# A second self-attention in stretches of scores, projections, scores and values on four double banks, with its ends and cross-attention's last element in another order

## The chip, the cores and the metric

The kernel runs on one core of one Trainium2 chip, in float32 throughout. Its time is the device time of one launch in microseconds (us). Three runs of the kernel before took 2361.93, 2363.57 and 2368.61 us; the median is 2363.57. A further execution was recorded by the hardware profiler: it took 2357.97 us, of which 2356.2 are the span from its first to its last instruction.

## What is computed

Two transformer blocks follow each other on x, 8 elements of 512 rows and 256 columns. The change is in the second block: its self-attention, and both ends of the cross-attention behind it.

```python
def _attn(xq, ctx, wq, wkv, wo, bo):          # H = 16 heads of DH = 64
    q = _heads(xq @ wq)
    k, v = jnp.split(ctx @ wkv, 2, axis=-1)
    k = _heads(k)
    v = _heads(v)
    sq, cq = _sincos(q.shape[2], DH)
    sk, ck = _sincos(k.shape[2], DH)
    q = _rope(q, sq, cq)
    k = _rope(k, sk, ck)
    sim = jnp.einsum('bhnd,bhmd->bhnm', q, k) * DH ** (-0.5)
    a = jax.nn.softmax(sim, axis=-1)
    o = jnp.einsum('bhnm,bhmd->bhnd', a, v)
    o = o.transpose(0, 2, 1, 3).reshape(xq.shape[0], xq.shape[1], MID)
    return o @ wo + bo
...
attn_in = _adaln(x, cond, ln1_w, ln1_b, g1_w, g1_b, b1_w, b1_b)
x = _attn(attn_in, attn_in, sa_wq, sa_wkv, sa_wo, sa_bo) + x
cross_in = _adaln(x, cond, ln1_w, ln1_b, g1_w, g1_b, b1_w, b1_b)
ctx_n = _ln(context, ca_lnc_w, ca_lnc_b)
x = _attn(cross_in, ctx_n, ca_wq, ca_wkv, ca_wo, ca_bo) + x
ffn_in = _adaln(x, cond, ln2_w, ln2_b, g2_w, g2_b, b2_w, b2_b)
h = jax.nn.gelu(ffn_in @ ff_w1 + ff_b1, approximate=False)
x = h @ ff_w2 + ff_b2 + x
```

## The kernel before

The kernel runs in stages on one core: the first block (its self-attention, cross-attention and feed-forward interleaved), then the second block's self-attention (class of work `batch4`, L991), then its cross-attention (`cross`, L1372) and its feed-forward (`feed_forward`, L1412). Almost every matrix product is issued in the helper `mm` (L117, L118), so the profile gives all of them one line; they are told apart by their tiles. In these stages TensorE, VectorE (DVE), ScalarE (ACT) and GpSimd (POOL) run in the order in which the program records their instructions (`manual_schedule`). The queue of SyncE (SP), which issues most DMAs, is ordered by the planner.

**Forms of a product.** TensorE's array holds 128 rows and 128 columns. A product over all of it is shown as `128*128`. Scores use it as four row strips, `32*128`: four heads, each with 32 of its 64 dimensions (the even or the odd half of the rotation), side by side. Values use column strips, `128*64`: two heads side by side. The sums of a softmax are `128*32`, four side by side. A float32 product is recorded as two matmuls.

**A group** is four heads, g = 0 to 3 for each element b. For each group there are queries and keys (`turned`, L1008: two products of 512 columns each into two PSUM banks; VectorE multiplies each by the cosine and the sine table into four tiles of tag t, L1016 and L1017; GpSimd combines them, L1019 and L1020), four blocks of scores by keys (`score(g, kt)`, L1028: eight matmuls into two double banks, and an exponential of 1024 columns each on ScalarE, L1037, into tiles p, of which there are six), and four blocks of values (`value(g, kt)`, L1039, four matmuls of 64 columns each into banks O and D). The sums over keys are first added up elementwise: p0 + p1 on GpSimd (L1052), then p2 and p3 on VectorE (L1056). `sums` (L1066) reduces them over partitions by a product with ones; ScalarE copies them, and they go through DRAM into another layout (`sums_back`), where VectorE inverts them (`inverse`, L1082), and through DRAM again, broadcast (`inverse_back`, rb). `scaled` (L1099) multiplies the values' output oT by them, both halves on GpSimd. `out_tiles` (L1104) projects the eight oT of an element.

**The order.** `slots` (L1161) goes through 64 slots of two score blocks. A slot issues a score block, then what the dictionaries `steps` and `mid` hold for it (projections, norm of the next element, output projection), then the next score block, then two value blocks, then what `after` holds (sums, the transposition of the next element by `transposed`, L423, through two X banks). After the last slot come the last sums, eight products for the values of cross-attention (`cross_values`, L973, one bank, one copy and one DMA of 256 KB each into v_d), the norms of the first elements, and the output projection of the last element.

**PSUM.** One pool serves the whole kernel: two double banks S, one bank each O and D, two banks X (L99 to L115).

**DRAM and SyncE.** `load_vb` (L965) reads back the values of one element for cross-attention from v_d into the tile kv or vb. The weights of the feed-forward, `ff_w1` and `ff_w2`, are loaded into the places of `ca_wv4` and `sa_wo` when these have had their last use.

**Cross-attention.** `cross` goes through j = 0 to 7 for each element b: scores in two halves (j = 0 and 4), queries six ahead, output of the element before (`cross_out(b - 1, t)`, j from 5), sums and inverse. The last element has no queries to go ahead with. Then `feed_forward` does four double products with Gelu (`up`) and four output tiles (`down`) an element; the last cross-attention output stands behind the first element's.

Of the kernel before, what the change touches and what calls it, by code (L numbers as in the profile page):

```python
# [10 lines left out]
F32 = mybir.dt.float32  # L11
# [76 lines left out]
def fast_path(ctx: ExitStack, tc: tile.TileContext, a: dict, out: bass.AP):  # L88
# [7 lines left out]
    psum = ctx.enter_context(tc.tile_pool(name="psum", bufs=2, space=bass.MemoryType.PSUM))  # L96
    turns, extra = [0], []

# [874 lines left out]
    def cross_values(wk, p):  # L973
        ps = bank_x()
        for k in range(2):
            mm(ps, cross["v"][:, k, p * P : (p + 1) * P], ctxzT[:, k, :], k == 0, k == 1)
        v = wk.tile([P, N], F32, tag=f"k{p % 2}", name="v")
        nc.scalar.copy(v, ps)
        nc.sync.dma_start(v_d[:, p], v.rearrange("p (b t) -> p b t", b=B))


    with tc.tile_pool(name="ph4", bufs=2) as wk:
# [3 lines left out]
        steps, mid, after = {}, {}, {}  # L986

        def last(slot, fn):
            steps.setdefault(slot, []).append(fn)

        def batch4(b):  # L991
            s = {}
            base = 2 * NG * b

            def turn():
                s["hT"] = transposed(nk, s["z"], b, a1, b1, 1)

            def values(half, ts):
                if ts[0] == 0:
                    s["v", half] = wk.tile([P, NT, 512], F32, tag="v", name="v")  # L1000
                for t in ts:
                    ps = bank_x()
                    for k in range(2):
                        mm(ps, s["hT"][:, k, t * P : (t + 1) * P], w_sv[:, k, half * 512 : (half + 1) * 512],
                           k == 0, k == 1)
                    nc.scalar.copy(s["v", half][:, t, :], ps)

            def turned(g, w, tag, pss=None):  # L1008

                even, odd = pss or (bank_x(), bank_x())  # L1010
                for e, ps in enumerate((even, odd)):
                    for k in range(2):
                        mm(ps, w[:, k, (2 * g + e) * P : (2 * g + e + 1) * P], s["hT"][:, k, :], k == 0, k == 1)
                ec, es, oc, os = (wk.tile([P, N], F32, tag="t", name="t", bufs=4) for _ in range(4))
                for ps, c, sn in ((even, ec, es), (odd, oc, os)):
                    nc.vector.tensor_tensor(c, ps, rope_c, ALU.mult)  # L1016
                    nc.vector.tensor_tensor(sn, ps, rope_s, ALU.mult)  # L1017
                s[tag, g] = r = [wk.tile([P, N], F32, tag=f"{tag}{e}", name=f"{tag}{e}") for e in range(2)]
                nc.gpsimd.tensor_tensor(r[0], ec, os, ALU.subtract)  # L1019
                nc.gpsimd.tensor_tensor(r[1], es, oc, ALU.add)  # L1020

            def queries(g, pss=None):
                turned(g, w_sq, "q", pss)

            def keys(g, pss=None):
                turned(g, w_sk, "k", pss)

            def score(g, kt):  # L1028
                pss = [bank_s() for _ in range(2)]
# [9 lines left out]
            def value(g, kt):  # L1039
                if kt == 0:  # L1040
                    s["o", 0], s["o", 1] = bank_o(), bank_d()
                for u in range(2):
                    p = 2 * g + u
                    for i in range(2):
                        lo = (p % 4) * P + 64 * i
                        mm(s["o", u][64 * i : 64 * i + 64, :], s["v", p // 4][:, kt, lo : lo + 64],
                           s["p", g, kt, u][:, i, :], kt == 0, kt == NT - 1)

                if kt == 0:
                    for u in range(2):  # L1050
                        s["sm", g, u] = sm = wk.tile([P, 2, N], F32, tag="sm", name="sm", bufs=4)
                        nc.gpsimd.tensor_tensor(sm, s["p", g, 0, u], s["p", g, 1, u], ALU.add)  # L1052
                if kt == 2:
                    for t in (2, 3):
                        for u in range(2):
                            nc.vector.tensor_tensor(s["sm", g, u], s["sm", g, u], s["p", g, t, u], ALU.add)  # L1056
                if kt == NT - 1:
                    for u in range(2):
                        s["oT", 2 * g + u] = o = wk.tile([P, N], F32, tag="oT", name="oT", bufs=10)
                        nc.scalar.copy(o, s["o", u])  # L1060


            def queue(g):
                return nc.scalar if (b, g) == (B - 1, NG - 1) else nc.sync

            def sums(g):  # L1066

                d = bank_x()
# [5 lines left out]
                queue(g).dma_start(dd, den.rearrange("(j r) n -> j r n", j=4)[:, 0, :])  # L1074
                if (b, g) != (B - 1, NG - 1):
                    sums_back(g)

            def sums_back(g):
                s["rec", g] = rec = wk.tile([P, 4 * N // P], F32, tag="rec", name="rec")
                queue(g).dma_start(rec, flat(s["dd", g]))  # L1080

            def inverse(g):  # L1082
                rec = s["rec", g]
                nc.vector.reciprocal(rec, rec)
                s["inv", g] = d = dram.tile([4, N], F32, tag="rec_d", name="rec_d")
                queue(g).dma_start(flat(d), rec)
                check(rec)
                if (b, g) != (B - 1, NG - 1):
                    inverse_back(g)

            def inverse_back(g):
                d = s["inv", g]
                for u in range(2):
                    s["rb", g, u] = rb = wk.tile([P, N], F32, tag="rb", name="rb", bufs=3)
                    for e in range(2):
                        queue(g).dma_start(rb[64 * e : 64 * e + 64, :],
                                           d[2 * u + e : 2 * u + e + 1, :].to_broadcast([64, N]))

            def scaled(g, engines=None):  # L1099
                for u, eng in enumerate(engines or [nc.gpsimd] * 2):  # L1100
                    o = s["oT", 2 * g + u]
                    eng.tensor_tensor(o, o, s["rb", g, u], ALU.mult)  # L1102

            def out_tiles(qp):  # L1104
                project_out(qp, lambda k: s["oT", k], w_so, 8, add_to(b))

            if b:

                pieces = normed_in_pieces(nk, b, EPS1, lambda z: s.update(z=z))
                last(base - 8, pieces[0])  # L1110
                last(base - 6, pieces[1])
                after[base - 6] = [pieces[2]]
                last(base - 5, lambda: add_row(b, row("sabo")))
                after.setdefault(base - 4, []).append(turn)
                last(base - 3, lambda: queries(0))
# [1182 lines left out]
```

## Time and profile before

| what | value |
|---|---|
| median of three runs | 2363.57 us |
| profiled execution | 2357.97 us |
| its span | 2356.2 us |
| first block, from 0 to | 826.7 us |
| second self-attention | 826.7 to 1814.0 us |
| cross-attention and feed-forward | 1814.0 to 2356.2 us |
| granted TensorE clock, mean | 0.999 |

Engine time in the stretch of the second self-attention, 827 to 1814 us:

| engine | busy us | instructions |
|---|---|---|
| TensorE | 985.51 | 4705 |
| VectorE | 500.49 | 624 |
| GpSimd | 523.49 | 276 |
| ScalarE | 357.19 | 440 |
| all DMA engines, share | 0.08 | |

Busy time of TensorE is modelled: matmuls are pipelined, and the end that is shown for one lies behind the start of the next. A busy TensorE is thus not one that streams all the time; how far apart its starts are tells more. Idle time of the other engines costs nothing by itself.

### The profile page before, as it was taken

Reading aid. Unit: us, or ns where it says so; the run is one execution under the profiler, and the core shown is the slowest. Engines: PE = TensorE matmul, PEld = TensorE weight load, DVE = VectorE, ACT = ScalarE, POOL = GpSimd, SP = SyncE. Lnnn points to the kernel's source line nnn. Section 1 sums busy time; section 2 is a strip of 40 time slices with the busy share of each in tenths; the row PEclk is TensorE's granted clock in tenths of the full one; section 3 lists DMA queues with packets and bytes.
Section 4 is the critical chain, followed back from the end, with each engine's and each line's share of the span. In section 5 each row is a group of like instructions: output and inputs, shape, how many; then the busy total and the mean of one; then the engine's idle time right before and its main releaser. Section 6 shows DMA issues by size and latency. Waiting matters only on the chain.

```text
span 2356.2 us, 29152 instructions
## 1 busy us (share of the span) xinstructions
PE 2336.6 (99%) x11348; PEld 1140.2 (48%) x11348; DVE 1073.4 (46%) x2043; ACT 885.2 (38%) x1118; POOL 945.0 (40%) x582
## 2 busy tenths in 40 slices
PE   9999999999999999999999999999999999999999
PEld 4333544544545643444444343434345556557666
DVE  4554544545335445555545454545444555532110
ACT  4665555555542134333333333333333221221221
POOL 4563223333201037554555555555453554531110
PEclk9999999999999999999999999999999999999999
DMA  5120000000003000000000000000113222220000
GB/s 188 38 105 11 17 16 9 17 17 7 11 14 98 1 1 20 19 20 19 19 19 20 19 19 19 19 20 11 35 58 103 71 79 70 66 66 23 18 23 20
DMA packets 84307, 83.85 MB, mean 36 GB/s; under 512 B 42192, under 2 KB 59328, under 8 KB 84160
## 3 DMA queue, kind: packets, MB, share of 16 engines
q1 hardware_dynamic: 82680, 78.73, 10.9%
q8 instruction: 91, 1.49, 0.2%
q0 software_dynamic: 576, 2.10, 0.2%
q10 hardware_dynamic: 904, 1.07, 0.1%
q14 instruction: 56, 0.46, 0.1%
HBM read 71.83 MB, written 10.04 MB: 35 GB/s over the span
## 4 chain that ended last, share of the span: by engine, by line
PE 96%; DMA 1%; DVE 1%; ACT 1%; issue 1%; POOL 0%; SPq 0%; ACTq 0%; DVEq 0%; POOLq 0%
PE ps_X L118 40%; PE ps_S L118 24%; PE ps_D L118 16%; PE ps_O L118 14%; PE ps_X L429 1%; DMA rb<-rec 1%; PE ps_X L616 1%; PE ps_X L576 0%; ACT p L596 0%; PE ps_D L616 0%; PE ps_D L429 0%; POOL var L567 0%; DMA rec<-rec 0%; PE ps_D L576 0%; ACT den L1072 0%
## 5 line engine op out<-in xcount | busy, mean ns | idle before, releaser
L118 PE MATMUL ps_S<-q,k 32*128 32x512 f32 (+1 forms) x3072 | 416.5, 622 | 2.5 <-ACT p L596 1.5
L1037 ACT ACTIVATE p<-ps_S 128x1024 f32<-128x1024 f32 x256 | 248.5, 1022 | 449.5 <-PE ps_S L118 449.2
L596 ACT ACTIVATE p<-ps_S 128x1024 f32<-128x1024 f32 x256 | 248.2, 1022 | 196.2 <-PE ps_S L118 195.4
L118 PEld LDWEIGHTS ps_S<-q,k 32*128 32x128 f32 (+1 forms) x3072 | 141.8, 184 | 228.1 <-issue 161.6
L1056 DVE TENSOR_TENSOR sm<-sm,p 128x1024 f32<-128x1024 f32 x128 | 251.3, 2022 | 0.2 <-ACT p L1037 0.2
L184 POOL TENSOR_TENSOR rstd<-rstd,mhalf 128x4 f32<-128x4 f32 x49 | 50.1, 1023 | 364.1 <-DVE rstd L183 363.5
L1019 POOL TENSOR_TENSOR q<-t 128x512 f32<-128x512 f32 x32 | 59.7, 1866 | 328.2 <-DVE t L1017 287.1
L1016 DVE TENSOR_TENSOR t<-ps_X,rope_c 128x512 f32<-128x512 f32 x126 | 86.9, 690 | 212.4 <-PE ps_X L118 212.2
L567 POOL TENSOR_TENSOR var<-var,mhalf 128x32 f32<-128x32 f32 (+1 forms) x17 | 87.4, 5141 | 171.3 <-DVE var L561 168.0
L1052 POOL TENSOR_TENSOR sm<-p 128x1024 f32<-128x1024 f32 x64 | 150.0, 2368 | 1.9 <-ACT p L1037 1.9
L118 PE MATMUL ps_X<-hT,w 128*128 128x512 f32 x328 | 150.4, 597 | 0.0
L1102 POOL TENSOR_TENSOR oT<-oT,rb 128x512 f32<-128x512 f32 x63 | 126.2, 2020 | 29.6 <-DMA rb<-rec_d 29.6
L118 PE MATMUL ps_O<-p,v 128*64 128x512 f32 x512 | 135.0, 606 | 0.0
L118 PE MATMUL ps_D<-p,v 128*64 128x512 f32 x512 | 131.6, 592 | 0.0
L118 PE MATMUL ps_O<-p,h 128*32 128x512 f32 x1024 | 129.6, 606 | 0.8 <-ACT p L596 0.8
L118 PE MATMUL ps_X<-w_sa_wv,hT 128*128 128x512 f32 x256 | 118.3, 605 | 0.0
L118 PE MATMUL ps_X<-hT,w_sa_wq 128*128 128x512 f32 x256 | 115.9, 596 | 0.0
L118 PE MATMUL ps_X<-w_sa_wo,oT 128*128 128x256 f32 x512 | 113.9, 381 | 0.6 <-DVE t L1017 0.5
L118 PE MATMUL ps_X<-hT,w_sa_wk 128*128 128x512 f32 x248 | 113.2, 599 | 0.0
L118 PE MATMUL ps_S<-hT,w_ff_w 128*128 128x512 f32 x256 | 111.3, 593 | 0.0
L118 PEld LDWEIGHTS ps_X<-w_sa_wo,oT 128*128 128x128 f32 x512 | 96.3, 190 | 22.6 <-issue 5.3
L1342 ACT ACTIVATE hid<-ps_S,cols 128x512 f32<-128x512 f32 x64 | 40.5, 684 | 176.3 <-PE ps_S L118 176.3
(284 smaller groups left out, 3481.9 us busy)
## 6 DMA issues: line engine op xcount, KB each, us to landing
rb<-rec SPq DMA_DIRECT2D x128, 128.0 KB
rb<-rec_d SPq DMA_DIRECT2D x124, 128.0 KB
rb<-rec SPq DMA_DIRECT2D x16, 256.0 KB
out_dram<-x SPq DMA_DIRECT2D x15, 256.0 KB
x<-in_x_dram SPq DMA_DIRECT2D x7, 512.0 KB
gate<-modd SPq DMA_DIRECT2D x24, 128.0 KB
k_d<-q POOLq DMA_DIRECT2D x4, 512.0 KB, 3.1
v_d<-v SPq DMA_DIRECT2D x8, 256.0 KB
```

Of the source, the lines that this page charges most:

```text
L118: nc.tensor.matmul(o, lhsT, rhs, start=start, stop=stop)
L184: nc.gpsimd.tensor_tensor(r[:, :n], r[:, :n], mhalf[:, :n], ALU.pow)
L429: nc.tensor.transpose(ps[:, t * P : (t + 1) * P], z[:, t, k * P : (k + 1) * P], ident)
L567: nc.gpsimd.tensor_tensor(var, var, half, ALU.pow)
L596: nc.scalar.activation(pr[u], pss[u], AF.Exp, scale=HD0 ** -0.5)
L1016: nc.vector.tensor_tensor(c, ps, rope_c, ALU.mult)
L1019: nc.gpsimd.tensor_tensor(r[0], ec, os, ALU.subtract)
L1037: nc.scalar.activation(pr, pss[u], AF.Exp, scale=HD1 ** -0.5)
L1052: nc.gpsimd.tensor_tensor(sm, s["p", g, 0, u], s["p", g, 1, u], ALU.add)
L1056: nc.vector.tensor_tensor(s["sm", g, u], s["sm", g, u], s["p", g, t, u], ALU.add)
L1102: eng.tensor_tensor(o, o, s["rb", g, u], ALU.mult)
L1342: nc.scalar.activation(s["hid"][:, f, :], ps[:, i, :], AF.Gelu, bias=col("ffb1")[:, f : f + 1])
```

## The change

Before the second self-attention the PSUM pool is closed and opened again, and all eight banks are given out as four double banks (`pair`). Afterwards it is opened once more with the former banks. The pools of PSUM and of both stages wait for single tiles when their space is used again (`reuse_waits="tile"`).

The dictionaries of slots are gone. Each group of four heads is issued as: two score blocks; the next group's queries, keys and a part of the values' projection (at one group of each element also the output projection of the element before, at another the transposition of the next); two score blocks; all four value blocks; sums. At the last group of an element the projections are those of the next element, and at the very last one a part of the cross-attention's values.

- A value block is eight matmuls of 32 columns (four side by side) in place of four of 64, into one double bank, which one copy of 1024 columns empties.
- Elementwise sums: the first pair of heads' three adds go to VectorE, the second pair's three to GpSimd.
- `turned` makes two products of 1024 columns in place of four of 512; its two tiles t are double. The first keys are combined on VectorE.
- `scaled` uses VectorE for the first half and GpSimd for the second.
- Transposition and output projection use one double bank each.
- The cross-attention's values are made two products at a time, four DMAs of 512 KB in place of eight of 256 KB. At the end of the stage six of the eight parts of the last output projection are issued between them.
- In cross-attention, two of the feed-forward's `up` of the first element stand at j = 2 and 3 of the last element, and the last sums before its inverse, at j = 6.

```diff
+    def pair():
+        return psum.tile([P, 2, 512], F32, tag="pair", name="ps_P", bufs=4)
...
+    other_banks()
+    with tc.tile_pool(name="ph4", bufs=2, reuse_waits="tile") as wk:
...
+            def turned(self, g, w, tag, ps=None, eng=nc.gpsimd):
...
+                c, sn = (wk.tile([P, 2, N], F32, tag="t", name="t") for _ in range(2))
+                nc.vector.tensor_tensor(c, ps, rope_c[:, None, :].to_broadcast([P, 2, N]), ALU.mult)
+                nc.vector.tensor_tensor(sn, ps, rope_s[:, None, :].to_broadcast([P, 2, N]), ALU.mult)
                 s[tag, g] = r = [wk.tile([P, N], F32, tag=f"{tag}{e}", name=f"{tag}{e}") for e in range(2)]
-                nc.gpsimd.tensor_tensor(r[0], ec, os, ALU.subtract)
-                nc.gpsimd.tensor_tensor(r[1], es, oc, ALU.add)
+                eng.tensor_tensor(r[0], c[:, 0, :], sn[:, 1, :], ALU.subtract)
+                eng.tensor_tensor(r[1], sn[:, 0, :], c[:, 1, :], ALU.add)
...
+            def add(self, g, kt):
+                s = self.s
+                for u, eng in enumerate((nc.vector, nc.gpsimd)):
+                    if kt == 1:
+                        s["sm", g, u] = wk.tile([P, 2, N], F32, tag="sm", name="sm", bufs=4)
+                        eng.tensor_tensor(s["sm", g, u], s["p", g, 0, u], s["p", g, 1, u], ALU.add)
+                    else:
+                        eng.tensor_tensor(s["sm", g, u], s["sm", g, u], s["p", g, kt, u], ALU.add)
...
+            def value(self, g):
+                s = self.s
+                ps = pair()
+                for kt in range(NT):
+                    for u in range(2):
+                        p = 2 * g + u
+                        for i in range(2):
+                            for h in range(2):
+                                lo = (p % 4) * P + 64 * i + 32 * h
+                                r = slice(64 * i + 32 * h, 64 * i + 32 * h + 32)
+                                mm(ps[r, u, :], s["v", p // 4][:, kt, lo : lo + 32], s["p", g, kt, u][:, i, :],
+                                   kt == 0, kt == NT - 1)
+                s["oT", g] = o = wk.tile([P, 2, N], F32, tag="oT", name="oT", bufs=5)
+                nc.scalar.copy(o, ps)
...
         def slots():
...
+                for g in range(NG):
+                    for kt in range(2):
+                        this.score(g, kt)
+                    this.add(g, 1)
+                    if g < NG - 1:
+                        jobs = [lambda: this.queries(g + 1), lambda: this.keys(g + 1)]
+                        if g == 1 and last:
+                            jobs.append(last.out)
+                        jobs.append(lambda: this.values((g + 1) // 2, 2 * (1 - g % 2)))
+                        if g == 2 and nxt:
+                            jobs.append(nxt.turn)
+                    elif nxt:
+                        jobs = [lambda: nxt.queries(0), lambda: nxt.keys(0), lambda: nxt.values(0, 0)]
+                    else:
+                        jobs = [lambda: cross_values(wk, 0)]
+                    for n, fn in enumerate(jobs):
+                        fn()
+                        if n == 0 and before:
+                            before[0].inverse(before[1])
+                        if n == 0 and nxt and g == 0:
+                            nxt.norm(0)
...
+                    for kt in (2, 3):
+                        this.score(g, kt)
+                        this.add(g, kt)
+                    this.value(g)
+                    if nxt and g < 2:
+                        nxt.norm(g + 1)
+                    if before:
+                        before[0].scaled(before[1])
+                    this.sums(g)
+                    before = this, g
+            end = todo[-1]
             first_rows.append(normed(nk, 0, EPS1))
             add_row(0, row("cabo"))
...
+            cross_values(wk, 1)
+            end.sums_back(NG - 1)
+            cross_values(wk, 2)
+            end.inverse(NG - 1)
+            end.inverse_back(NG - 1)
+            end.last_out(range(6))
+            cross_values(wk, 3)
             load_vb(0)
+            end.scaled(NG - 1)
+            first_rows.append(pair_turned(first_rows[0], 0))
...
+            end.last_out((6, 7))
...
+    other_banks()
...
+                    if b == B - 1 and j in (2, 3):
+                        up(0, j - 2)
...
                     if j == 6:
+                        if b == B - 1:
+                            sums(b, 1)
                         inverse(b, 0)
-            sums(B - 1, 1)
...
-                for ff in range(4):
+                for ff in range(0 if b else 2, 4):
                     up(b, ff)
-                    if b == 0 and ff < 3:
-                        (lambda: scaled(B - 1, 0), lambda: inverse(B - 1, 1), lambda: scaled(B - 1, 1))[ff]()
+                    if b == 0:
+                        (scaled if ff == 2 else inverse)(B - 1, ff - 2)
+                if b == 0:
+                    scaled(B - 1, 1)
```

## The prediction

> **What bounds the kernel now.** I read the page first: engines, chain of waits, groups. Then the waits of TensorE, and the time-ordered rows of TensorE, VectorE, GpSimd and the SyncE queue in four places.
>
> ```profile
> PE 2336.6 (99%) x11348; PEld 1140.2 (48%) x11348; DVE 1073.4 (46%) x2043; ACT 885.2 (38%) x1118; POOL 945.0 (40%) x582
> ...
> PE 96%; DMA 1%; DVE 1%; ACT 1%; issue 1%; POOL 0%; SPq 0%; ACTq 0%; DVEq 0%; POOLq 0%
> ```
>
> TensorE carries the time, and no other engine is half busy. A shorter time therefore needs fewer TensorE microseconds or fewer TensorE waits. The list of waits leaves little of the second kind: in the whole second self-attention it holds one of 0.5 us. So the question is what TensorE does with its 987.3 us there (first query projection 826.68, first cross-attention query 1813.96). Starts of consecutive rows say it better than busy times, since ends are modelled:
>
> ```profile
> 603.89 3.60 PE L118 MATMUL ps_X<-hT,w 128*128 128x512 f32 x8
> 607.33 1.88 PE L118 MATMUL ps_D<-hT,w 128*128 128x512 f32 x4
> ...
> 610.21 1.92 PE L118 MATMUL ps_O<-p,h 128*32 128x512 f32 x16
> 612.06 0.66 PE L616 MATMUL ps_X<-ident,oT 128*128 128x128 f32 x4
> ```
>
> Eight full-array passes follow the same form and take 607.33 - 603.89 = 3.44 us, 0.43 each. (Each f32 matmul is recorded twice: two passes.) Four 32-column matmuls side by side are one "wave": 16 records are 4 waves and take 1.85 us, 0.13 over 4 x 0.43.
>
> ```profile
> 1019.70 2.00 PE L118 MATMUL ps_S<-q,k 32*128 32x512 f32 x16
> 1021.63 3.70 PE L118 MATMUL ps_X<-hT,w_sa_wk 128*128 128x512 f32 x8
> 1025.26 2.00 PE L118 MATMUL ps_S<-q,k 32*128 32x512 f32 x16
> 1027.19 1.08 PE L118 MATMUL ps_O<-p,v 128*64 128x512 f32 x4
> ...
> 1030.78 1.07 PE L118 MATMUL ps_X<-sm,ones 128*32 128x512 f32 x8
> ```
>
> One slot of the stage. A scores run of 4 waves takes 1.93 us, 0.21 over streaming; a projection run of 8 takes 3.63, 0.19 over; values, 8 waves, 3.59, 0.15 over; sums, 2 waves, 0.99, 0.13 over. **Each change of form costs a fixed 0.13 to 0.21 us**, however long the run is. That is what the change can take.
>
> **Part 1, fewer changes of form.** Streaming first: 1888 waves of 512 columns (512 scores, 512 values, 512 queries and keys, 256 values' projections, 64 sums, 32 cross values) x 0.4294 = 810.7; 512 output passes x 0.2158 = 110.5; 64 transposes x 0.109 = 7.0; 928.2 us. The stage took 987.3, so 59.1 is not streaming. Of the two programs' orders on TensorE, before has 297 changes of form, after 129. Before: 297 x 0.186 (mean of the four prices in that mix) = 55.2; the other 3.9 are small waits, 8 x 0.26 of them between the two halves of a transposition. After, a group of four heads is scores (0.21), projections (0.19), scores (0.21), values with sums as one run of 18 waves (0.13 to 0.14): 0.75 x 32 = 24.0, with the ends 24.6. **Gain 30.6 us**, and about 2.6 of the small waits, since the transposition now has both halves in one tile.
>
> The values go from 512 matmuls of 64 columns to 1024 of 32. [...] The row above has this very form, four abreast, at 0.43 a wave, as two of 64 columns have. I take the row: nothing[...].
>
> **Part 2, the four double banks.** All of TensorE's outputs now rotate through four tiles, and whoever empties one holds TensorE. I walk one group, t = 0 at the first score, with durations of rows: exponentials of 1024 columns 0.92 apart (1.02 each), VectorE's rotation products 0.60 per 512 columns from PSUM, GpSimd's rotations 1.27, its adds 2.37, VectorE's add 1.2. TensorE: scores to 3.65, queries to 7.2, keys to 10.6, values' projection to 14.05, scores to 17.8, values to 24.7, sums to 25.7. Queries need the first exponential (3.1; 0.5 to spare). The third tile of the second scores stretch sits where the keys were: VectorE's products of the keys wait for GpSimd's rotation of the queries (only two product tiles now) and end at 14.7; wanted at 16.0. The seventh exponential needs a p buffer (six, eight made) that the values free at 18.9; it ends at 19.9, the eighth at 20.85; wanted at 23.0 and 23.9. Sums want the third add of both engines, and here it is tight:
>
> ```profile
> 1015.50 8.95 DVE L1056 TENSOR_TENSOR sm<-sm,p 128x1024 f32<-128x1024 f32 x4
> ...
> 1015.76 2.10 POOL L1019 TENSOR_TENSOR q<-t 128x512 f32<-128x512 f32 x1 [12.87 <-DVE t L1017]
> ```
>
> Four VectorE adds took 8.95 us instead of 4.8, and the rotation beside them 2.10 instead of 1.27[...]. So GpSimd's second add runs 18.35 to 20.7, VectorE's third to 21.9, GpSimd's third to 24.2; sums are due at 24.7. Half a microsecond is left: **no stall, cost 0**; if that cover goes, each further 0.1 us a group costs 3.2. ScalarE has 8 exponentials, two copies and the values' copy a group, some 11 us of 25.7, and is not late anywhere. Moved with the adds: inverse (its DMA round trip is back by 4.3, it stands behind the queries' products at 9.75) and scaled, which now follow the adds on both engines; nobody waits for them until the output projection, half a group later at the least. The norm's pieces and its row add (GpSimd, 2.35 us, 3.34 beside an add) now stand behind a group's last add too; GpSimd has nothing else due from 24.2 until the next group's first add at 31.6, so they cost nothing; in front of an add they would cost their length.
>
> **Part 3, the start.** The first tile lies on the bank of the last feed-forward output, which VectorE reads until 827.3; TensorE would start at 826.7: 0.7 us lost. Scores then start behind queries, keys and values (838.1); the keys' rotation, now on VectorE, is done at 837.9.
>
> **Part 4, the end of the stage.** The last softmax inverse has more cover than before (two cross values and 48 output matmuls): no cost. But the order of SyncE's queue changes.
>
> ```profile
> 1798.58 0.38 SPq L166 DMA_DIRECT2D w_ff_w<-in_ff_w_dram  x1
> 1799.39 0.79 SPq L979 DMA_DIRECT2D v_d<-v  x2
> 1808.02 1.22 SPq L968 DMA_DIRECT2D kv<-v_d  x2
> 1814.15 0.39 SPq L166 DMA_DIRECT2D w_ff_w<-in_ff_w_dram  x1
> 1814.71 0.54 SPq L963 DMA_DIRECT2D kb<-k_d  x1
> ```
>
> Before, the last cross values ended 15.4 us before the stage's end T, and their way through DRAM (weights and v_d out, 9.4 us to the kv issue, 3 to landing) was done by T - 3. After, they end at T - 4.3, and SyncE has the second feed-forward weight, which waits for the last use of the output weights at T, ahead of kv. With the 9.5 us from there to the kv issue (1798.52 to 1808.02) that is T + 5.2; the broadcasts of the last inverse, which kept the DMA engines busy until 1799, now run 10 us earlier and take about 1.4 off: issue near T + 3.8, landed 3 later near T + 7; the first product with kv is due at T + 3.4. **A new wait of 3.6 us** (2 to 5), with nothing behind it to fill TensorE.
>
> **Part 5, cross-attention's last element.**
>
> ```profile
> 2094.55 1.25 PE L118 MATMUL ps_D<-vw,p 128*128 128x256 f32 x4 [2.15 <-POOL p L1314]
> 2096.83 0.70 PE L118 MATMUL ps_D<-vw,p 128*128 128x256 f32 x2 [1.03 <-POOL p L1314]
> ```
>
> From 2090.40 to 2101.85 TensorE takes 11.45 us for 7.0 of streaming: 4.4 of waiting for the scaled probabilities, as the last element has no queries to project. The two feed-forward pieces moved ahead of sums there are 6.9 us, more than the wait, and the broadcasts stay ahead in SyncE's queue: the wait goes. They cost something: the second score tile now waits for the second Gelu, 0.5 us; ScalarE loads its tables for Exp and Gelu twice more (1.28 each at 2110.7), beside TensorE work. The last scaled probabilities come due 47 us after those pieces, ready at 38. **Gain 3.9.**
>
> **Sum.** -30.6 - 2.6 + 0.7 + 3.6 - 3.9 = -32.8, say -33. The span of 2356.2 becomes 2323, the profiled execution's 2357.97 becomes 2325. The runs shown have a median of 2363.57, 5.6 above the profiled one; the difference is carried over: **2330.5 us**.
>
> **Rivals.** (A, 0.79) the forecast; its unknowns (start 0 to 1, kv 2 to 5, the residual waits 0 to 2.6, a tenth of a microsecond at the adds) give 2324 to 2337. (B, 0.12) sums wait for GpSimd. For: its adds grow from two to three a group, beside VectorE's; the margin is 0.5. Against: rotations are done before. If both adds meet a VectorE add, sums are 0.6 late: 32 x 0.6 = 19, 2349. (C, 0.06) slower: the two product tiles. If GpSimd's rotations take 2.25 as they did beside adds, the keys' products end at 16.7, 0.7 too late for the scores, the keys' rotation at 21, and the adds behind it 1.5 to 2 too late for sums: some 1.5 us a group, 48 us: 2378. It decides from 1.03 us a group (32.8 / 32) on. Against it: VectorE adds nothing in that window, since adds stand before 6.2 or after 17. (D, 0.03) the price belongs not to the change of form but to something each run does (a semaphore): then fewer, longer runs save half[...]. Against: queries followed by values' projections, two runs of one form, are 0.43 apart like the rest.
>
> Less than 0.3% (7.1 us) can't be told from no change. A and B are faster, D nearly none, C slower: 0.91, 0.03, 0.06. From 2321 to 2348 leaves out C, D and half of B.
>
> **What would show it.** In the changed profile: scores runs of 8 waves at 3.65 us, values and sums at 7.9 in one; stage near 954 us; no TensorE wait at sums (a wait there on GpSimd is B); a hole of 2 to 5 us before the first product with kv, released by a DMA; no hole in the last element's output. A wait of scores on VectorE's products in every group would make the prediction wrong.

## The result, and the profile after

The changed kernel takes 2329.72 us (median of 4 runs, 2327.45 to 2332.87) against 2363.54 (4 runs) for the kernel before: ratio 0.9854, 95% interval 0.9835 to 0.9873. A second set of runs of the same two kernels gave 2331.29 against 2363.66, 0.9872 (0.9855 to 0.9889). The forecast was 2330.5 us, in a range of 2321 to 2348. The profiled execution took 2329.47 us, where 2325 were forecast.

First the page of the changed kernel: engines, then two groups (busy us, mean ns, idle before).

```profile
span 2327.7 us, 30865 instructions
...
PE 2304.4 (99%) x12372; PEld 1150.3 (49%) x12372; DVE 996.6 (43%) x1911; ACT 870.7 (37%) x1052; POOL 918.4 (39%) x581
...
L128 PE MATMUL ps_P<-q,k 32*128 32x512 f32 x2048 | 237.8, 601 | 1.4 <-DVE k L1047 1.4
L1075 POOL TENSOR_TENSOR sm<-sm,p 128x1024 f32<-128x1024 f32 x64 | 174.9, 2733 | 141.5 <-ACT p L1066 141.4
```

TensorE is 99% busy as before and has 1024 more records, yet the span is 28.5 us shorter. So nothing moved off TensorE: its own work takes less time. One group of four heads on TensorE in the changed kernel, in order of time (start, modelled length):

```profile
866.62 3.72 PE L128 MATMUL ps_P<-q,k 32*128 32x512 f32 x32
870.27 3.70 PE L128 MATMUL ps_P<-hT,w_sa_wq 128*128 128x512 f32 x8
873.81 3.60 PE L128 MATMUL ps_P<-hT,w_sa_wk 128*128 128x512 f32 x8
877.24 3.60 PE L128 MATMUL ps_P<-w_sa_wv,hT 128*128 128x512 f32 x8
880.77 3.71 PE L128 MATMUL ps_P<-q,k 32*128 32x512 f32 x32
884.41 7.07 PE L128 MATMUL ps_P<-p,v 128*32 128x512 f32 x64
891.30 1.04 PE L128 MATMUL ps_P<-sm,ones 128*32 128x512 f32 x8
892.27 3.29 PE L128 MATMUL ps_P<-q,k 32*128 32x512 f32 x28
```

Read the distances between starts. Eight waves of scores take 870.27 - 866.62 = 3.65 us (two runs of four took 3.86), values and sums 892.27 - 884.41 = 7.86 as one run. No row carries a wait. The waits that are left stand in the list of TensorE's waits (total us, times, longest):

```profile
PE ps_O L128 <- DMA kv<-v_d: 4.8, 1, 4.8
...
PE ps_P L128 <- DVE k L1047: 1.4, 1, 1.4
PE ps_P L128 <- DVE tmp L805: 0.5, 1, 0.5
```

The first is the hole (a stretch in which TensorE has nothing to do) ahead of the first product with kv, one element's values read back from DRAM. The second is a wait of the very first scores, the third the bank at the start. I split each trace at two points that every kernel has, the first query projection of the second self-attention and the first query of cross-attention, and at the start of the last matmul:

| us | before | after | difference |
|---|---|---|---|
| up to the second self-attention | 826.68 | 828.98 | +2.30 |
| the second self-attention | 987.28 | 953.88 | -33.40 |
| from the first cross-attention query to the last matmul | 536.31 | 538.12 | +1.81 |
| behind the last matmul | 5.91 | 6.70 | +0.79 |
| span | 2356.18 | 2327.68 | -28.50 |

The stage gains what was forecast (954). The forecast gain at cross-attention's last element and the forecast wait for kv meet in the third row, which needs experiments.

### The profile page after: what moved, and what is told of

It reads as the page before. It is cut to its first block, busy times and chain, and to the rows that moved or that the text cites. A ratio compares the mean times of both kernels' runs of the same rounds, so it can differ in the third digit from the quotient of the medians.

```text
span 2327.7 us, 30865 instructions
## 1 busy us (share of the span) xinstructions
PE 2304.4 (99%) x12372; PEld 1150.3 (49%) x12372; DVE 996.6 (43%) x1911; ACT 870.7 (37%) x1052; POOL 918.4 (39%) x581
## 4 chain that ended last, share of the span: by engine, by line
PE 96%; DMA 1%; DVE 1%; issue 1%; ACT 1%; POOL 0%; SPq 0%; POOLq 0%; ACTq 0%; DVEq 0%
PE ps_P L128 40%; PE ps_X L128 21%; PE ps_S L128 13%; PE ps_D L128 10%; PE ps_O L128 9%; PE ps_X L439 1%; PE ps_X L626 1%; DMA rb<-rec 0%; PE ps_X L586 0%; ACT p L606 0%; PE ps_D L439 0%; DMA v_d<-v 0%; PE ps_P L1005 0%; PE ps_D L626 0%; POOL var L577 0%
## 5 line engine op out<-in xcount | busy, mean ns | idle before, releaser
L606 ACT ACTIVATE p<-ps_S 128x1024 f32<-128x1024 f32 x256 | 248.2, 1022 | 196.2 <-PE ps_S L128 195.5
L1066 ACT ACTIVATE p<-ps_P 128x1024 f32<-128x1024 f32 x256 | 245.0, 1026 | 94.8 <-PE ps_P L128 94.8
L128 PE MATMUL ps_P<-q,k 32*128 32x512 f32 x2048 | 237.8, 601 | 1.4 <-DVE k L1047 1.4
L1075 POOL TENSOR_TENSOR sm<-sm,p 128x1024 f32<-128x1024 f32 x64 | 174.9, 2733 | 141.5 <-ACT p L1066 141.4
L128 PE MATMUL ps_P<-p,v 128*32 128x512 f32 x2048 | 226.4, 594 | 0.0
L1075 DVE TENSOR_TENSOR sm<-sm,p 128x1024 f32<-128x1024 f32 x64 | 97.7, 1526 | 152.3 <-ACT p L1066 152.3
L128 PE MATMUL ps_S<-q,k 16*128 16x512 f32 x1024 | 160.0, 640 | 2.5 <-ACT p L606 1.5
L128 PE MATMUL ps_P<-hT,w_sa_wq 128*128 128x512 f32 x256 | 118.4, 606 | 0.5 <-DVE tmp L805 0.5
L128 PE MATMUL ps_P<-hT,w_sa_wk 128*128 128x512 f32 x256 | 115.1, 593 | 0.0
L128 PE MATMUL ps_P<-w_sa_wv,hT 128*128 128x512 f32 x256 | 115.1, 592 | 0.0
```

The lines of the kernel that those rows point to most:

```text
L128: nc.tensor.matmul(o, lhsT, rhs, start=start, stop=stop)
L606: nc.scalar.activation(pr[u], pss[u], AF.Exp, scale=HD0 ** -0.5)
L1066: nc.scalar.activation(pr, pss[u], AF.Exp, scale=HD1 ** -0.5)
L1075: eng.tensor_tensor(s["sm", g, u], s["sm", g, u], s["p", g, kt, u], ALU.add)
```

## The experiments

"Stage" and "tail" are the second and third row of that table; they are read from one trace each, and repeat better than the time of a run (the changed kernel's second trace: stage 953.88, tail 538.74). Medians are of 4 to 11 runs.

**1. Values in 64 columns again.** Does the number of matmuls cost, or the change of form?

```diff
-    for h in range(2):
-        lo = (p % 4) * P + 64 * i + 32 * h
-        r = slice(64 * i + 32 * h, 64 * i + 32 * h + 32)
-        mm(ps[r, u, :], s["v", p // 4][:, kt, lo : lo + 32], ...
+    lo = (p % 4) * P + 64 * i
+    mm(ps[64 * i : 64 * i + 64, u, :], s["v", p // 4][:, kt, lo : lo + 64], ...
```

> The changed kernel with the values again as 512 matmuls of 64 columns in two-fold packing instead of 1024 of 32 columns in four-fold packing; everything else as changed. My theory (a change of form costs, the number of matmuls does not): the values take the same 8 waves a pass, and their own form adds one change per group before the sums: 32 x 0.15 = +4.7 us, profiled about 2334. [...]

Median 2335.64 us (the profiled execution, 2340.15, lies above the 2334 expected through the first block; see the end). The stage takes 958.70, 4.82 more than 953.88, with 1024 records fewer. TensorE in this kernel:

```profile
1007.77 7.09 PE L128 MATMUL ps_P<-p,v 128*64 128x512 f32 x32
1014.79 1.06 PE L128 MATMUL ps_P<-sm,ones 128*32 128x512 f32 x8
1015.78 3.72 PE L128 MATMUL ps_P<-q,k 32*128 32x512 f32 x32
```

Values and sums take 1015.78 - 1007.77 = 8.01 us, 0.15 more than in four-fold packing: the sums are a run of their own. 32 x 0.15 is the difference. A price of each matmul would have made this version the faster one, and none shows: from the values to the sums it is 1014.79 - 1007.77 = 7.02 us here, in 32 records, and 891.30 - 884.41 = 6.89 in 64, and the 0.13 between them is most of that 0.15. Four matmuls of 32 columns side by side cost what two of 64 cost.

**2. The first scores stretch split again.** Same matmuls, same banks, same widths.

```diff
-                    for kt in range(2):
-                        this.score(g, kt)
-                    this.add(g, 1)
+                    this.score(g, 0)
...
                         fn()
+                        if n == 0:
+                            this.score(g, 1)
+                            this.add(g, 1)
```

> The changed kernel with the first two score tiles of a group apart again: score 0, queries, score 1, keys, values' projection, then as before; the same matmuls, the same banks, the same widths. My theory (each run of one form costs 0.21 us for scores and 0.19 us for projections): one more scores run and one more projection run per group, 32 x 0.40 = +12.8 us, profiled about 2342. Rival (the gain came from the double banks or the wider instructions, not from longer runs): no change, 2329 to 2330. Runs of 4 waves of scores should again take 1.93 us where a run of 8 takes 3.65.

Median 2345.96 us; stage 967.57, +13.69. TensorE in this kernel:

```profile
1011.82 2.00 PE L128 MATMUL ps_P<-q,k 32*128 32x512 f32 x16
1013.75 3.70 PE L128 MATMUL ps_P<-hT,w_sa_wq 128*128 128x512 f32 x8
1017.38 2.00 PE L128 MATMUL ps_P<-q,k 32*128 32x512 f32 x16
1019.31 3.70 PE L128 MATMUL ps_P<-hT,w_sa_wk 128*128 128x512 f32 x8
1022.85 3.60 PE L128 MATMUL ps_P<-w_sa_wv,hT 128*128 128x512 f32 x8
```

The runs of four waves take 1.93 us again, the projections behind them 3.63 and 3.54. There are 62 more runs (the very last group has no second projection to split off), at 13.69 / 62 = 0.22 each, a tenth over the forecast. TensorE's list of waits for the stage is that of the changed kernel, so no new stall is in it. With double banks, wide instructions and the new order of adds all in place, the split alone gives 13.7 of the 33.4 us back; that the rest has the same price follows by multiplication, 33.4 / (297 - 129) = 0.20 for each change of form that went.

This experiment alone adds runs and changes of form together, so it can't tell the theory from rival D (each run has a price of its own). Two other readings can. In the group shown above, queries, keys and values' projection are three runs of one form: from the keys to the values' projection it is 877.24 - 873.81 = 3.43 us, eight waves with nothing over, and all three take 10.50, 0.19 over streaming, as much as one projection alone. And experiment 1 leaves the sums right behind the values, as the changed kernel has them; they cost 0.15 more there, where the two differ in form. The change of form is the cause, and rival D falls. What happens in the array at a change is not shown.

**3. The last cross values ahead of the output matmuls.** The wait for kv.

```diff
+            cross_values(wk, 3)
+            load_vb(0)
             end.last_out(range(6))
-            cross_values(wk, 3)
-            load_vb(0)
```

> The changed kernel with the last cross values (and the load of vb behind them) put ahead of the 48 output matmuls of the last self-attention element instead of behind them; the same instructions. The kv load then stands ahead of the second feed-forward weight on SyncE. My theory: the wait of 4.8 us before the first product with kv goes, and with it the half clock that follows it (about 1.5 us): -6.5 us, profiled about 2323, and no granted clock under 1 near 1791. Rival 1 (the wait only moves: the next transfers are late instead, or the weight's load now arrives late): 0 to -2 us. Rival 2 (the half clock has another cause and stays): -5 us, with the clock still at 0.5 there.

Median 2325.13 us, ratio 0.984 (0.982 to 0.986). Stage 953.88, unchanged; tail 532.06, 6.06 less than with the hole. In the changed kernel SyncE's queue and the DMA engines looked so (the last two columns of the second view are the DMA engines' busy share and GB/s, the one before the granted clock):

```profile
1779.81 0.32 SPq L990 DMA_DIRECT2D v_d<-v  x1
1783.06 0.38 SPq L176 DMA_DIRECT2D w_ff_w<-in_ff_w_dram  x1
1786.19 1.22 SPq L978 DMA_DIRECT2D kv<-v_d  x2
1787.50 0.58 SPq L973 DMA_DIRECT2D kb<-k_d  x1
```

```profile
1784.00:1786.00 2.00, 2.00 (x6) 0.76 (x4) 0.84 (x3) 0.00 (x0) 0.62 (x1) 1.00 1.01 364
1786.00:1788.00 2.00, 0.46 (x2) 0.00 (x0) 1.71 (x3) 0.00 (x0) 0.00 (x0) 1.00 1.04 348
1788.00:1790.00 2.00, 0.00 (x0) 0.00 (x0) 0.78 (x2) 0.00 (x0) 1.08 (x1) 1.00 1.25 202
1790.00:1792.00 2.00, 0.74 (x2) 0.68 (x3) 0.00 (x0) 0.00 (x0) 1.40 (x2) 0.69 0.57 80
```

The kv load (256 KB) is issued 3.1 us behind the second feed-forward weight of 1 MB, and all DMA engines are busy with that weight when it is. Another load of 256 KB, kb, follows 1.3 us behind kv. In the trace the weight's packets run until 1788.8 us and those of kv and kb together from 1787.8 to 1791.4, so kv shares the engines first with the one and then with the other. With the values first, SyncE and the DMA engines of that version:

```profile
1779.84 1.22 SPq L978 DMA_DIRECT2D kv<-v_d  x2
1785.71 0.39 SPq L176 DMA_DIRECT2D w_ff_w<-in_ff_w_dram  x1
```

```profile
1780.00:1782.00 2.00, 2.00 (x15) 1.80 (x14) 0.00 (x0) 0.00 (x0) 0.45 (x1) 1.00 0.30 68
1782.00:1784.00 2.00, 2.00 (x12) 1.77 (x10) 1.66 (x6) 1.45 (x2) 0.20 (x1) 1.00 0.28 63
```

Here kv goes ahead of both, over engines that are 0.3 busy with kv included, and TensorE's first product with it starts 3.84 us behind the first query, 0.4 over streaming. Nothing later is late instead: rival 1 falls. That the values stand behind the output matmuls is thus shown as the cause of the hole. Moved ahead, kv is issued 9 us earlier against the first query and finds the engines free; no run takes the two apart, nor the weight's part from kb's.

**4. The pools' option left out.**

```diff
-    ... name="psum", bufs=2, space=bass.MemoryType.PSUM, reuse_waits="tile"))
+    ... name="psum", bufs=2, space=bass.MemoryType.PSUM))
```

> The changed kernel without the pools' option by which a new tile waits only for its own predecessor (in all places where the change set it). My theory: it carries nothing of the gain: 0 to +1 us, 2329 to 2331. Rival (part of the gain is that option's): +5 us or more, with waits in front of score runs that the changed kernel doesn't have.

Median 2329.54 us, no difference. But the traces are not alike; TensorE in this kernel:

```profile
1789.20 1.95 PE L128 MATMUL ps_X<-hT,w_ca_wq 128*128 128x512 f32 x4 [2.07 <-DVE x L1145]
...
1795.77 1.10 PE L128 MATMUL ps_O<-w_ca_wo,kv 128*128 128x256 f32 x4 [2.90 <-DMA kv<-v_d]
```

Without the option the first cross query waits 2.07 us for VectorE's last output, so the stage grows to 956.20, and the hole before kv shrinks by nearly as much. The tail is 534.86, 3.26 less: 1.9 for the shorter hole, and the clock stays whole behind it (1.00 from 1794 to 1802 us; experiment 6). What the option saves was covered by the wait for kv.

**5. The cross-attention part alone**, in the kernel before.

```diff
+                    if b == B - 1 and j in (2, 3):
+                        up(0, j - 2)
...
                     if j == 6:
+                        if b == B - 1:
+                            sums(b, 1)
                         inverse(b, 0)
-            sums(B - 1, 1)
```

(The feed-forward loop starts behind the two pieces moved, as in the change.)

> The kernel before with the cross-attention part of the change alone (feed-forward pieces 0 and 1 in the last element's loop, its sums ahead of the inverse). My theory: the wait of 4.4 us for the scaled probabilities goes and at most 0.5 comes back at the second score tile, so the stretch from the first cross query to the last matmul takes 536.31 - 3.9 to - 4.4 = 531.9 to 532.4 us, and the profile about 2354; the median some 4 us under before's. Rival (the freed time is given back in the feed-forward part that follows, which lost its own cover): 536 in that stretch, no change.

Median 2357.43 against 2363.39 us, 0.9973 (0.996 to 0.9986). Stage 987.29, as before; tail 531.96, 4.35 less than 536.31. The whole wait of 4.4 is gained, nothing comes back. (The profiled execution, 2359.24, missed the 2354 expected in the first block; see the end.)

**6. The hole filled** with matmuls whose results nobody reads.

```diff
                 queries(n)
+                if n == 1:
+                    spare = bank_s()
+                    for _ in range(5):
+                        mm(spare[:, 0, :], ident, turned_rows[0][:, 0, :])
```

> The changed kernel with five needless matmuls (ten records of 512 columns, 4.3 us; results unused) put into the hole before the first product with kv, which waits for a transfer all the same. My theory (the half clock behind the hole comes from TensorE's idle time): the clock stays at 1 near 1791, the product starts at the same time, and the stretch from the first cross query to the last matmul takes 538.1 - 1.5 = 536.6 us. Rival 1 (the half clock comes from elsewhere): still 0.5 there, 538.1. Rival 2 (the added matmuls are in the way of kv): over 539.

Median 2330.80 us, which can't be told from 2329.72. The traces can. TensorE in the changed kernel, then in this one:

```profile
1784.58 1.88 PE L128 MATMUL ps_D<-hT,w_ca_wq 128*128 128x512 f32 x4
1791.26 2.04 PE L128 MATMUL ps_O<-w_ca_wo,kv 128*128 128x256 f32 x4 [4.80 <-DMA kv<-v_d]
1793.10 2.41 PE L128 MATMUL ps_X<-hT,w_ca_wq 128*128 128x512 f32 x4
1795.35 1.03 PE L128 MATMUL ps_X<-w_ca_wo,kv 128*128 128x256 f32 x4
```

```profile
1790.13 4.46 PE L128 MATMUL ps_S<-hT,ident 128*128 128x512 f32 x10
1795.03 1.10 PE L128 MATMUL ps_O<-w_ca_wo,kv 128*128 128x256 f32 x4 [0.45 <-issue]
1795.97 1.88 PE L128 MATMUL ps_X<-hT,w_ca_wq 128*128 128x512 f32 x4
```

Four matmuls with kv take 1793.10 - 1791.26 = 1.84 us behind the hole and 0.94 behind the filler. The tail is 536.63, 1.49 less, as expected; the granted clock stays at 1.00 in every slice. In the changed kernel it is 0.50 from 1792 to 1794 us: the idle time itself costs clock afterwards.

**7. VectorE's third add on GpSimd too**: the cover of the sums.

```diff
-    eng.tensor_tensor(s["sm", g, u], s["sm", g, u], s["p", g, kt, u], ALU.add)
+    (nc.gpsimd if kt == 3 else eng).tensor_tensor(s["sm", g, u], ...
```

> The changed kernel with VectorE's third add of a group on GpSimd too, so that GpSimd has four adds behind one another and ends later. It prices the margin of the sums: GpSimd ended its last add 0.65 us before them in the changed kernel. My theory (GpSimd is the next bound, with 0.65 us of cover): one add of 2.4 us more, less 0.6 since nothing of VectorE's is beside it, is 1.2 us late a group: 32 x 1.2 = +38 us (to +56 if the add keeps its 3.0), stage 992 to 1010 us, with a TensorE wait on GpSimd at every sums. Rival (the cover is larger, other work takes the place at sums): under +10 us.

Median 2369.27 us; stage 991.46, +37.58 or 1.17 a group. GpSimd, then TensorE:

```profile
1011.79 7.21 POOL L1075 TENSOR_TENSOR sm<-sm,p 128x1024 f32<-128x1024 f32 x3 [14.74 <-ACT p L1066]
```

```profile
1018.15 1.95 PE L128 MATMUL ps_P<-sm,ones 128*32 128x512 f32 x8
1020.03 3.71 PE L128 MATMUL ps_P<-q,k 32*128 32x512 f32 x32
```

The third add ends at 1019.0, in the middle of the sums: the wait lies between the first and the second half of that run (1.88 us from start to start, where 0.97 is usual), so the row shows none in front of it; TensorE's list has only 24 such waits, 5.6 us in all, and the starts tell more. The gain of the whole change hangs on less than one add of cover.

**8 and 9. The start.** To experiment 3 a third product tile is added (room from one tile of broadcast inverses); then GpSimd's first row add is moved as well.

```diff
-    c, sn = (wk.tile([P, 2, N], F32, tag="t", name="t") for _ in range(2))
+    c, sn = (wk.tile([P, 2, N], F32, tag="t", name="t", bufs=3) for _ in range(2))
...
             first.queries(0)
-            add_row(0, row("sabo"))
...
                     this.sums(g)
+                    if (b, g) == (0, 0):
+                        add_row(0, row("sabo"))
```

> The changed kernel with the last cross values ahead of the output matmuls, as in the run that moved them, and with three product tiles instead of two (one of the three tiles of broadcast inverses given up for the room). My theory of the start: the first scores wait because the keys' products find both product tiles held until GpSimd has rotated the queries; with a third tile the keys' first product starts 1.2 us earlier, the wait of 1.6 us before the first scores shrinks to 0.3 to 0.5, and the stage takes 953.9 - 1.2 = 952.7 us; no other place changes; profile about 2322 to 2324. Rival (the start waits for VectorE itself): stage 953.9. Rival 2 (two tiles of inverses are too few): a wait of VectorE or GpSimd in every group, stage over 956.

> The version with the last cross values ahead and three product tiles, and with GpSimd's first row add (2.35 us) moved from behind the first queries to behind the first group's sums. In the run with three product tiles the keys' products were 1.1 us earlier, but VectorE's first rotation of the keys took 1.57 us instead of 0.69, beside that row add. My theory[...]: the rotation takes 0.69 again, the first scores start 0.9 us earlier, their wait falls from 1.4 to 0.5, the stage takes 953.63 - 0.9 = 952.7 us and the profile about 2321 to 2323; no effect elsewhere. Rival (the rotation is slow for another reason): 1.57 again, stage 953.6. Rival 2 (the row add is in the way in its new place): the rotations of the second group are late and the stage takes 954 or more.

The third tile alone: median 2324.38 us, stage 953.63, only 0.25 less; this expectation was missed. With the row add moved: median 2324.36, stage 952.75, as expected. VectorE in the changed kernel, with three tiles, and with the row add moved:

```profile
837.74 1.22 DVE L1044 TENSOR_TENSOR t<-ps_P,rope_c 128x1024 f32<-128x1024 f32 x1 [2.66 <-POOL q L1048]
838.88 1.21 DVE L1045 TENSOR_TENSOR t<-ps_P,rope_s 128x1024 f32<-128x1024 f32 x1
840.13 0.69 DVE L1047 TENSOR_TENSOR k<-t 128x512 f32<-128x512 f32 x1
```

```profile
837.58 1.23 DVE L1044 TENSOR_TENSOR t<-ps_P,rope_c 128x1024 f32<-128x1024 f32 x1 [1.08 <-PE ps_P L128]
839.17 1.23 DVE L1045 TENSOR_TENSOR t<-ps_P,rope_s 128x1024 f32<-128x1024 f32 x1 [0.37 <-POOL q L1048]
840.43 1.57 DVE L1047 TENSOR_TENSOR k<-t 128x512 f32<-128x512 f32 x1
```

```profile
842.96 0.69 DVE L1047 TENSOR_TENSOR k<-t 128x512 f32<-128x512 f32 x1
```

And GpSimd's row add, with three tiles:

```profile
839.10 2.35 POOL L460 TENSOR_TENSOR x<-x,rows 128x1024 f32<-128x1024 f32 x1
```

First kernel: VectorE stands 2.66 us, until GpSimd has rotated the queries and both product tiles are free. With a third tile only the second product waits (0.37), but then the rotation comes to lie beside that row add (839.10 to 841.45) and takes 1.57 us instead of 0.69. With that add gone it takes 0.69. From the first query projection to the first scores the three kernels need 11.99, 11.74 and 10.86 us; 10.4 are streaming.

**10. The changed kernel again**, on the same chip as 9.

> The changed kernel as it is, on the same chip as the version with the three moves, for a direct comparison: median 2329.7, profile 2327 to 2333, and again the hole of 5 us before the first product with kv with the clock at half behind it, stage 953.9 and from the first cross query to the last matmul 538.1 us. The version with the moves should stand 6 to 8 us under it.

Median 2331.29, tail 538.74, the half clock there again; version 9 stands 6.9 us (0.3%) under it, at 0.9833 (0.9819 to 0.9846) of the kernel before. It is the fastest measured here, level with 8.

## Why the prediction was right, point by point

**Part 1 (gain 30.6 and 2.6): right.** In the stage 953.88 - 928.2 of streaming - 1.6 of waiting at the start leave 24.1 us for 129 changes of form, 0.187 each if nothing else is in it; the prediction had 0.186 and 1.3 us of small waits besides. Experiments 1 and 2 priced two kinds of run by themselves, 0.15 and 0.22. No run takes the 2.6 us of small waits apart from the rest. That twice as many matmuls of half the width cost nothing, taken from a row of before, held (experiment 1).

**Part 2 (no stall): right.** GpSimd's last add of a group ended 0.63 to 0.67 us before the sums in nearly all 32 groups (0.5 forecast). In the group shown above it ends at 890.66, and the sums start at 891.30:

```profile
887.63 3.03 POOL L1075 TENSOR_TENSOR sm<-sm,p 128x1024 f32<-128x1024 f32 x1 [0.29 <-ACT p L1066]
```

That the adds of the two engines follow one another was an estimate. In the trace they overlap and take longer: VectorE's third add, from 1003.89 us, 1.80 us where its second took 1.23, GpSimd's third, from 1004.92, 3.00 where its second took 2.43. Experiment 7 shows that this cover is real and what stands behind it, 1.17 us a group, so rival B's wait exists, beyond the margin. Rival C doesn't: with a third product tile nothing changes in the groups, only at the start.

**Part 3 (0.7 lost, scores not late): half right.** The bank cost 0.7 (0.5 of it listed as a wait). The step that failed is "the keys' rotation, now on VectorE, is done at 837.9": Part 2 had said that there are two product tiles and that the keys' products wait for GpSimd's rotation of the queries, and Part 3 left it out. The scores were 1.6 us late; experiments 8 and 9 show the tiles, and the row add behind them, as the cause.

**Part 4 (a new wait of 3.6): right in its place, too small.** The place and the releaser are as named, and the issue came at T + 3.3 (T is the end of the stage; 3.8 forecast). The term that was mis-sized is "landed 3 later". The trace of before had kv on DMA engines that carried nothing else, and its last packet ended 2.9 us behind the issue:

```profile
1808.00:1810.00 2.00, 2.00 (x11) 1.77 (x10) 1.28 (x2) 0.00 (x0) 1.70 (x2) 1.00 0.28 64
```

Here it shared them with the 1 MB weight in front and kb behind. The product started 5.1 us behind the issue, 5.0 us late; by these figures, as an estimate, 2.8 of the 5.0 come from the late issue (3.3 + 2.9 - 3.4) and 2.2 from the shared engines. The second part of the miss has no term at all in the sum: the half clock behind the hole, 1.5 (experiment 6). Of these 6.5 us experiment 3 gains 6.06; 0.4 stays without the hole, too.

**Part 5 (gain 3.9): right, 0.45 too careful.** The gain is 4.35. The 0.5 for the second score tile is no new cost: these scores took 2.43 us before and take 2.31 after. TensorE at the last element of the changed kernel shows the hole gone, 32 records of the output in 7.1 us:

```profile
2070.11 2.38 PE L128 MATMUL ps_S<-q,kb 32*64 32x512 f32 x32
2072.42 7.17 PE L128 MATMUL ps_X<-vw,p 128*128 128x256 f32 x32
2079.52 1.07 PE L128 MATMUL ps_X<-p,sel 128*32 128x512 f32 x8
```

**The sum.** The span fell by 28.5 us where 32.8 were forecast. The 4.3 are: 2.1 in the tail (2.5 too little for kv, less 0.45), 0.8 behind the last matmul, 1.6 ahead of the stage over the forecast 0.7, and -0.2 in the stage, where the late scores and the small waits, gone altogether, cancel. The 1.6 and the 0.8 lie where the instructions are the same, and vary from one execution to the next: the second trace of the changed kernel starts the stage at 828.15 and has 5.54 behind the last matmul, and the one wait that is longer in front of the stage (1.33 us from start to start at 764.47 before, 2.00 after) is 1.96 in experiment 5, which has before's instructions there. The half clock of the last section is not the cause of the 1.6: both traces have one stretch of it, 3.41 us, ahead of the stage. No other cause was sought. That the median (33.8 under before's) came out nearer than the profile is luck of that kind: the profiled execution of before was among its fastest, that of after near its median.

## What to carry to other kernels

On a TensorE that is always busy, count runs, not matmuls: a change between row-tiled, column-tiled and full-array matmuls cost 0.15 to 0.22 us here where it was priced by itself, and fewer runs were worth most of the stage's 33 us while cutting values into twice as many matmuls cost nothing. When work is moved, redo the walk for the first and the last pass by themselves, with the same limits as in the steady state (tiles, queue order, bytes already in flight): both misses of the prediction were there. Price a load by what shares the DMA engines with it, in front and just behind: kv's last packet ended 2.9 us behind the issue on engines that carried nothing else, and 5.1 us passed to the first product with it when it shared them. Price a hole on TensorE by the slow matmuls behind it as well: behind the one of 4.8 us four matmuls took 1.84 us instead of 0.94.

## What the runs showed of the hardware that was not expected

**The granted clock halved behind five of the holes.** In the changed kernel the granted clock is 0.5 from 1790.75 to 1794.16 us, for 3.41 us, behind the hole of 4.8 us; with the hole filled (experiment 6) it is 1 there. Where the traces were read in slices of 0.2 us, the half clock up to the last matmul lasts 3.41, 6.83 or 10.24 us, which is one, two or three times 3.413, and its stretches in one trace begin whole multiples of that apart: 1621.33 us in the changed kernel (475 times), 64.85, 20.48 and 1624.75 in experiment 1 (19, 6 and 476). So they lie on a grid of 3.41 us in these traces, and the holes can be laid on it:

| trace | hole, us | TensorE busy in the emptiest 3.41 us of the grid | half clock behind it, us |
|---|---|---|---|
| changed kernel | 4.8 | 0% | 3.41 |
| experiment 10 | 5.3 | 0% | 3.41 |
| experiment 1 | 5.7 | 0% | 6.83 |
| experiment 2 | 5.2 | 0% | 6.83 |
| experiment 7 | 4.3 | 28% | 3.41 |
| experiment 4 | 2.1 and 2.9 | about 50% (an estimate) | none |

For experiment 4 the grid was laid from its clock of 0.70 between 80 and 100 us and 0.96 between 100 and 120, taken as one stretch of 13.65. In the first 3.41 us at half clock TensorE was busy for 85, 91 and 100% in the changed kernel and experiments 10 and 7, where no more followed, and for 44 and 81% in experiments 1 and 2, where another 3.41 did. The length of a hole alone does not order them: 5.3 us stood ahead of 3.41 (experiment 10), 5.2 ahead of 6.83 (experiment 2). No run moved a hole on the grid by itself, and why the clock changes there is not shown.

**Half clock goes with much of the spread between executions.** The later the second self-attention starts in a trace, the more of the first 180 us was at half clock, in a part of the kernel that is the same in all of them but for the PSUM pool's option (experiment 4). It starts at 826.7 to 829.0 us in the four traces with 3.41 us of it, at 830.4 with 6.83, at 831.6 with 10.24, at 832.8 to 833.1 with 13.65 (five traces, that of experiment 5 among them) and at 834.3 with 17.07 (experiment 1). Where it was read in slices of 0.2 us (before, the changed kernel, experiments 1, 3 and 5), TensorE was busy for 63 to 100% of the 3.41 us ahead of such a stretch, so no empty stretch like the one ahead of kv stands in front of them; what starts them was not tried.

**Beside the same GpSimd add VectorE was slower over some operands and not over others.** VectorE's rotation from two tiles in SBUF took 1.57 us instead of 0.69 beside GpSimd's row add (experiment 8); its products from PSUM took 1.22 and 1.21 beside the same add in the changed kernel (837.67 to 840.02), as they do without it (1.23 and 1.22 in experiment 9).
